# Finishing the all-node units of layers 2 and 3 earlier, and projecting front tiles first in layer 2

## The chip, the core and the metric

The kernel runs on one core of a Trainium2 chip. The core has a matrix engine (TensorE, PE in the profile; its weight loads are listed apart as PEld), a vector engine (VectorE, DVE), a scalar engine for functions such as exponentials (ScalarE, ACT), GpSimd (POOL), which here issues gathers, and SyncE (SP), whose queue issues the ordinary DMA transfers. The engines run side by side. Each takes its own instructions from its own list and they wait for one another on semaphores. The metric is the time of the whole kernel on the device in microseconds; the time before is 2346.93 us, the median of three runs (2338.59 to 2347.44).

## The reference

There are 4096 nodes with 256 features. The graph is a 4096 x 4096 adjacency matrix; an entry is set with a chance of 1 in 256, and the diagonal always. Four graph-attention layers follow one another, and each is wrapped in the same way:

```
x = layernorm(x + layer_n(x, adj))
```

Cut to its core, a layer does this for every node `i`:

```
h = x @ W
e[i, j] = leaky_relu(s[i] + d[j])          # s, d: h (or x) times short vectors
a[i, :] = softmax(where(adj[i, :], e[i, :], -inf))
out[i] = sum_j a[i, j] * h[j]
```

Layers 0 and 1 have four heads of 64 features and layer 2 has two heads of 128. Layer 3 has one head of 256 but two softmaxes, one of `e` and one of `-e`; both averages go through a matrix and `elu`. A node has some 16 neighbours, so the sum over `j` is sparse.

## The kernel before, in words

Nodes are handled in 32 row tiles of 128. For each row tile the kernel builds, during layer 0, a list of the nodes that are a neighbour of any of its 128 rows: 13 groups of 128 nodes. With the tile's own rows, which need no gather, that makes 14 positions. The six groups at the front hold only nodes of tiles 0 to 16 (`MIX = 17`), and these are called front nodes and front tiles here. The lists and masks are reused by all layers.

**A row tile** (`RowTile`) is worked in two halves of seven positions. `load` (lines 614 to 631) issues the DMA transfers of a half: for 13 positions of the 14 a gather on GpSimd (line 629) brings 128 rows of the projected values into a slot of the pool `g0` (16 slots; in layer 2 a slot holds two positions, so a tile takes 7; in layer 3 a slot holds one, and the second half's positions come from `g1`, 14 slots). The own rows come by SyncE's queue (line 626). `half` (lines 633 to 682) makes the weights: exponentials on ScalarE (line 670 in layer 2, lines 657 to 660 in layer 3), masks on VectorE (line 671, and 659 and 661), and then 14 matmuls on TensorE (line 682). After both halves, `finish` (lines 973 to 996) divides by the softmax sums on VectorE, adds the input and calls `norm` (lines 928 to 961), a chain of some twenty short VectorE instructions ending in line 956, which puts the tile into the list `ready`.

**All-node units** (`whole_rows`, lines 866 to 919) are a second way to compute the same thing. For the last `WHOLE[n]` blocks of four row tiles, the kernel doesn't gather: it runs over all 32 node tiles, with plain loads (line 888), exponentials over 512 columns (lines 900, and 903 to 907), one mask (lines 901 and 908), and matmuls (line 911). One node tile is a unit. Layer 2 has three such blocks, which makes 96 units of 8 matmuls, and layer 3 has one block, which makes 64 units of 4 matmuls (32 for each sign). So layer 2 has 20 row tiles with gathers and 12 without, layer 3 has 28 and 4. Gathers are GpSimd's work, and units need none.

**The order.** Layers 2 and 3 go through `half_with_whole` (lines 791 to 814) once for each half of a row tile: half step `2 m + part`. One half step makes at most one projection for the next layer (from `ready`, in the order of entry), one half of a row tile, the finish of the tile before, and as many units as `whole` (lines 736 to 742) allows: a share of all units that grows evenly and is complete 6 half steps before the layer's last one. After a block's last unit its four tiles are finished too and enter `ready`.

**A projection** (`Projection`, lines 520 to 591) takes a finished row tile to the values that the next layer gathers: transposes on TensorE (line 532), a copy on ScalarE (537), matmuls (546), an exponential (564), VectorE's part of the row (566 to 572) and the store of the row to HBM (574), and a small transposed store of its edge terms (578 to 585).

**The boundary.** `close` (lines 821 to 863) ends a layer: first the projections of front tiles that are left, then the first loads and gathers of the next layer, then the last tile's finish and the other projections. A gather of front groups needs the projected rows of tiles 0 to 16 only; any other gather needs those of all 32 tiles.

The Python loop isn't the last word: a scheduler places the instructions of each engine in an order of its own when the program is built, by readiness and its own estimates. On the chip each engine then keeps that order.

Of the kernel before, what the change touches and what calls it, by code (L numbers as in the profile page):

```python
# [76 lines left out]
MIX = 17  # L77
# [16 lines left out]


WHOLE = (0, 0, 3, 1)

LEAST = 2.0611536224385579e-09

# [35 lines left out]
def kernel(ctx: ExitStack, tc: tile.TileContext, ins: dict, out: bass.AP):  # L135
# [14 lines left out]
        "maskW": dram.tile([NB, P, NT, BT, MC], U8, name="maskW"),  # L150
        "d": [const.tile([P, NT, TERMS[n]], F32, name=f"d{n}") if WHOLE[n] else None for n in range(4)],
        "v": [dram.tile([N, ROW[n]], F32, name=f"vals{n}") for n in range(4)],
# [34 lines left out]
class Program:  # L187
# [97 lines left out]
    def lists(self, ctx):  # L285
# [71 lines left out]
        class Block:  # L357
# [24 lines left out]
            def places(self):  # L382
                blk = self.blk
                if blk >= NB - max(WHOLE):
                    nc.sync.dma_start(out=shared["maskW"][blk], in_=self.mk)
# [134 lines left out]
class Projection:  # L520
# [36 lines left out]
    def row(self):  # L557
# [8 lines left out]
        nc.vector.tensor_copy(self.terms[:, :, :A], st[:, :, :A])  # L566
        if WHOLE[n]:
            nc.vector.tensor_copy(sh["d"][n][:, m, :], st[:, 1, :])
# [136 lines left out]
class Layer:  # L705
# [3 lines left out]
    def __init__(self, prog, n):  # L709
        self.prog, self.n, self.nc, self.shared = prog, n, prog.nc, prog.shared  # L710
        self.count = NT - WHOLE[n] * BT
        self.tiles = {}
        self.loaded = set()
        self.units = self.whole_rows()
        self.total = WHOLE[n] * NT * (1 if n < 3 else 2)
        self.used = 0
# [18 lines left out]

    def whole(self, step):

        while self.used < self.total and self.used < self.total * (step + 1) / (2 * self.count - 6):
            next(self.units)
            self.used += 1  # L740
        if self.used == self.total:
            next(self.units, None)

    def part(self, m, part):


        if part == 0:
# [3 lines left out]
            for q in (m, m + 1):  # L751
                for half in range(2):
                    self.load(q, half)
        if WHOLE[self.n]:
            self.half_with_whole(m, part)
# [35 lines left out]
    def half_with_whole(self, m, part):  # L791

        proj = None
        self.step = 2 * m + part
        if self.ready and self.ready[0][0] < self.step:
            _, y, row = self.ready.pop(0)
            self.set_banks()
            proj = Projection(self.prog, self.n + 1, self.nxt, y, row)
            proj.transpose()
        if part == 1 or self.tile(m).accs is None:  # L800
            self.tile(m).half(part)
        if self.stored is not None:
            self.stored.store()
            self.stored = None
        if proj is not None:
            proj.copy()
            proj.multiply()
        if part == 1 and m >= 1:
            self.tile(m - 1).finish()
        self.whole(2 * m + part)  # L810
        if proj is not None:
            proj.row()
            proj.edge()
            self.stored = proj
# [643 lines left out]
```

## Time and profile before

| what | us |
|---|---|
| median of three runs | 2346.93 |
| span of the profiled run | 2346.8 |
| layer 2: first half's matmuls begin | 1364.7 |
| layer 2: last matmul of a unit ends | 1763.7 |
| layer 2: last gather ends | 1779.1 |
| layer 2: last matmul of a half ends | 1800.2 |
| layer 3: first gather (front groups) begins | 1811.6 |
| layer 3: gathers of the other groups begin | 1845.5 |
| layer 3: last matmul of a unit ends | 2287.0 |
| layer 3: last gather ends | 2311.0 |
| layer 3: last matmul ends | 2334.4 |

| engine | busy us | share of the span |
|---|---|---|
| TensorE, matmuls | 2052.4 | 87% |
| TensorE, weight loads | 1864.7 | 79% |
| VectorE | 1838.1 | 78% |
| ScalarE | 1747.3 | 74% |
| GpSimd | 1582.6 | 67% |

The shares are averages over layers that have different limits, so the table of times is the one to keep in mind: it cuts the last 1000 us at the places where something ends or begins. In a line of the timeline, the numbers are the start and the length in us; then follow the engine, the line of the kernel, the instruction with its output and inputs, how many were merged, and in brackets the idle time of the engine just before it with what ended it. An fp32 matmul of the code appears as two records.

### The profile page before, as it was taken

The numbers are of one execution on the slowest core, as the hardware profiler recorded it, in microseconds if no ns is written. First come the engines' busy times: TensorE is split into PE (matmuls) and PEld (weight loads), VectorE is DVE, ScalarE is ACT, GpSimd is POOL, SyncE is SP. The second block draws the span as 40 slices with busy tenths as digits, with TensorE's granted clock in tenths as the row PEclk, the third lists the DMA queues.
The fourth block names the chain that finished last, engine by engine and source line by source line (L and its number), as shares of the span: only waits on it lengthen the run. The fifth ranks groups of instructions, "written<-read, shape, count | busy, mean of one in ns | idle before, by whom it ended". The sixth has DMA issues, their size and how long they took to land.

```text
span 2346.8 us, 49828 instructions
## 1 busy us (share of the span) xinstructions
PE 2052.4 (87%) x15689; PEld 1864.7 (79%) x15689; DVE 1838.1 (78%) x6100; ACT 1747.3 (74%) x5137; POOL 1582.6 (67%) x1596
## 2 busy tenths in 40 slices
PE   4878898989988769999999889889898799979996
PEld 3668788888888759988888879888887688868885
DVE  3889999999987759989899859876866365656567
ACT  4779898897787749988888859877663666666663
POOL 2127887777788757777777767755553677777773
PEclk7999999999999979999999989999999899989998
DMA  8889687775555556666666657666665788888883
GB/s 278 267 269 322 220 284 255 245 268 155 157 140 159 148 168 182 190 176 170 174 175 183 167 147 202 200 187 188 187 179 150 248 250 276 268 245 267 272 251 119
DMA packets 250325, 492.01 MB, mean 210 GB/s; under 512 B 44385, under 2 KB 156610, under 8 KB 249666
## 3 DMA queue, kind: packets, MB, share of 16 engines
q0 software_dynamic: 81536, 245.30, 37.1%
q1 hardware_dynamic: 168514, 243.42, 32.5%
q8 instruction: 126, 2.06, 0.4%
q14 instruction: 149, 1.22, 0.2%
HBM read 436.24 MB, written 52.31 MB: 208 GB/s over the span
## 4 chain that ended last, share of the span: by engine, by line
PE 47%; DVE 20%; DMA 18%; ACT 8%; issue 4%; POOL 3%; SPq 0%; ACTq 0%; DVEq 0%; POOLq 0%
PE bank L679 17%; PE bank L682 12%; DMA G<-vals,idx 12%; PE bank L911 7%; PE bank L546 5%; DVE w L671 5%; PE bank L436 4%; DMA G<-vals 3%; POOL G L629 3%; DVE w L666 3%; DVE w L667 3%; ACT w L670 3%; DVE oh L430 2%; DMA raw<-in_adjB_dram 2%; ACT pw L900 1%
## 5 line engine op out<-in xcount | busy, mean ns | idle before, releaser
L629 POOL DMA_INDIRECT G<-vals,idx x1456 | 1569.6, 1078 | 718.5 <-issue 188.1
L670 ACT ACTIVATE w<-S,G 128x128 f32<-128x128 f32 x3248 | 1009.6, 391 | 204.7 <-DMA G<-vals,idx 194.6
L679 PE MATMUL bank<-w,G 128*65 128x128 f32 x7168 | 846.8, 279 | 94.9 <-DVE w L667 65.0
L679 PEld LDWEIGHTS bank<-w,G 128*65 128x65 f32 x7168 | 810.4, 142 | 109.8 <-DVE w L667 84.5
L682 PE MATMUL bank<-G,w 128*128 128x257 f32 (+1 forms) x2688 | 499.4, 344 | 34.8 <-ACT z L970 11.5
L682 PEld LDWEIGHTS bank<-G,w 128*128 128x128 f32 x2688 | 439.2, 196 | 84.7 <-ACT z L970 13.9
L671 DVE SCALAR_TENSOR_TENSOR w<-w,mk 128x896 f32<-128x896 f32 x272 | 292.6, 1082 | 42.8 <-ACT w L670 42.1
L911 PE MATMUL bank<-vw,pw 128*128 128x129 f32 (+1 forms) x2048 | 304.8, 306 | 14.3 <-ACT zw L970 13.0
L911 PEld LDWEIGHTS bank<-vw,pw 128*128 128x128 f32 x2048 | 279.4, 195 | 32.0 <-ACT zw L970 13.4
L666 DVE TENSOR_SCALAR w<-S,G 128x128 f32<-128x128 f32 x896 | 238.7, 298 | 80.0 <-DMA G<-vals,idx 78.9
L657 ACT ACTIVATE w<-S,G 128x128 f32<-128x128 f32 x392 | 137.9, 389 | 146.6 <-DMA G<-vals 96.6
L546 PE MATMUL bank<-wext,xT 128*128 128x268 f32 (+3 forms) x640 | 188.3, 427 | 49.7 <-ACT xT L537 45.9
L430 DVE TENSOR_SCALAR oh<-iota,place 128x256 bf16<-128x256 f16 (+2 forms) x992 | 223.7, 298 | 8.3 <-PE bank L436 7.9
L671 DVE SCALAR_TENSOR_TENSOR w<-w,bank 128x896 f32<-128x896 f32 x192 | 206.0, 1078 | 8.9 <-ACT w L670 8.8
L436 PE MATMUL bank<-mk,oh 128*128 128x132 fp8e4 x2336 | 188.7, 228 | 15.7 <-DVE oh L430 8.7
L436 PEld LDWEIGHTS <-oh 128*128 128x128 bf16 x2336 | 147.3, 100 | 51.3 <-DVE oh L430 23.5
L546 PEld LDWEIGHTS bank<-wext,xT 128*128 128x128 f32 x640 | 122.0, 208 | 72.8 <-ACT xT L537 50.8
L908 DVE TENSOR_TENSOR pw<-pw,mw 128x512 f32<-128x512 f32 x64 | 43.9, 690 | 137.8 <-ACT pw L907 71.2
L901 DVE SCALAR_TENSOR_TENSOR pw<-pw,mw 128x512 f32<-128x512 f32 x192 | 127.8, 687 | 21.2 <-ACT pw L900 19.8
L373 ACT ACTIVATE mk<-raw 128x1024 uint8<-128x1024 int32 x128 | 131.5, 1063 | 16.9 <-DMA raw<-in_adjB_dram 16.5
L900 ACT ACTIVATE pw<-Sw,d 128x512 f32<-128x512 f32 x192 | 132.9, 708 | 3.4 <-PE bank L911 3.2
L443 ACT ACTIVATE cm<-bank 128x384 uint8<-128x384 f32 (+1 forms) x160 | 70.1, 451 | 60.4 <-PE bank L436 58.4
(131 smaller groups left out, 1710.5 us busy)
## 6 DMA issues: line engine op xcount, KB each, us to landing
raw<-in_adjB_dram SPq DMA_DIRECT2D x128, 512.0 KB
mk<-maskC SPq DMA_DIRECT2D x112, 224.0 KB
G<-vals,idx POOLq DMA_INDIRECT x1456
S<-edge SPq DMA_DIRECT2D x64, 256.0 KB
vw<-vals SPq DMA_DIRECT2D x96, 129.0 KB
xp<-y SPq DMA_DIRECT2D x96, 128.0 KB
y<-xp SPq DMA_DIRECT2D x96, 128.0 KB
mw<-maskW SPq DMA_DIRECT2D x20, 528.0 KB
```

What stands on the lines that cost most here:

```text
L430: nc.vector.tensor_scalar(oh[:, :n * P], iota[:, :n * P], self.place[:, it, j:j + 1], None, op0=ALU.is_equal)
L436: nc.tensor.matmul(accs[b][:, s * MC:(s + 1) * MC], oh[:, (k - a) * P:(k - a + 1) * P], mk[:, j, it, :].bitcast(FP8), start=touches[b][0] ...
L546: nc.tensor.matmul(pp[:, :c1 - c0], self.xT[:, k, :], wext[:, k, c0:c1], start=(k == 0), stop=(k == KT - 1 and brow is None))
L629: nc.gpsimd.indirect_dma_start(out=self.place(pos), out_offset=None, in_=sh["v"][n][:NODES[t], :], in_offset=bass.IndirectOffsetOnAxis(ap= ...
L657: nc.scalar.activation(w[0][:, k, :], S[:, 0, :], AF.Relu, bias=d(k, 0))
L666: nc.vector.tensor_scalar(w[h][:, k, :], S[:, h, :], d(k, h), LEAST, op0=ALU.mult, op1=ALU.max)
L670: nc.scalar.activation(w[h][:, k, :], S[:, h, :], AF.Exp, bias=d(k, h))
L671: nc.vector.scalar_tensor_tensor(w[h], w[h], LEAST, mh, op0=ALU.max, op1=ALU.mult)
L679: nc.tensor.matmul(accs[0][:Wd, h * P:(h + 1) * P], v, w[h][:, k, :], **how)
L682: nc.tensor.matmul(a, w[h][:, k, :], v, **how)
L900: nc.scalar.activation(p, S[:, h], AF.Exp, bias=d)
L911: nc.tensor.matmul(accs[it][:, c:c + Wd], p[:, it, :], v[:, c:c + Wd], start=(j == 0 and h == heads[0]), stop=(j == NT - 1), skip_group_ch ...
```

## The change

The number of half steps that are left when the units are used up becomes one for each layer: 12 for layer 2 and 10 for layer 3, in place of 6 for both. The 96 units of layer 2 are then spread over 28 half steps (34 before) and the 64 of layer 3 over 46 (50 before). This is to have the blocks without gathers finished, and their tiles projected, before the layer's last tiles are. The second part concerns the choice of the next projection: among the tiles in `ready` that may go, front tiles are taken ahead of others (Python's sort keeps the order of entry among equals). It bears on layer 2 alone, since layer 3 projects nothing. It is to let the next layer's front gathers start without waiting for the rows of tiles 17 to 31. No instruction is added or removed; only their order differs.

```diff
 WHOLE = (0, 0, 3, 1)
+LAST = (0, 0, 12, 10)
...
     def whole(self, step):
 
-        while self.used < self.total and self.used < self.total * (step + 1) / (2 * self.count - 6):
+
+        while self.used < self.total and self.used < self.total * (step + 1) / (2 * self.count - LAST[self.n]):
             next(self.units)
             self.used += 1
...
         self.step = 2 * m + part
-        if self.ready and self.ready[0][0] < self.step:
-            _, y, row = self.ready.pop(0)
+
+        able = sorted((e for e in self.ready if e[0] < self.step), key=lambda e: e[2] >= MIX)
+        if able:
+            self.ready.remove(able[0])
             self.set_banks()
-            proj = Projection(self.prog, self.n + 1, self.nxt, y, row)
+            proj = Projection(self.prog, self.n + 1, self.nxt, *able[0][1:])
             proj.transpose()
```

## The prediction

> **What bounds the kernel now.** I read the chain of waits first: TensorE heads it (47%), by the matmuls of lines 679, 682 and 911, but gathers (line 629) stand in it too. A share over 2347 us says little about two stages, so I cut layers 2 and 3 into stretches.
>
> ```profile
> PE 47%; DVE 20%; DMA 18%; ACT 8%; issue 4%; POOL 3%; SPq 0%; ACTq 0%; DVEq 0%; POOLq 0%
> ...
> 1680.00:1750.00 70.00, 63.88 (x495) 60.73 (x494) 53.16 (x149) 50.55 (x135) 38.62 (x38) 0.95 0.63 179
> 1750.00:1790.00 40.00, 33.20 (x251) 31.36 (x251) 24.95 (x117) 18.82 (x60) 20.92 (x21) 0.96 0.57 163
> 1790.00:1820.00 30.00, 25.51 (x128) 19.92 (x127) 17.29 (x97) 9.53 (x24) 6.54 (x7) 0.89 0.53 158
> ...
> 2100.00:2200.00 100.00, 100.00 (x463) 87.67 (x462) 58.36 (x169) 63.81 (x136) 77.32 (x75) 1.00 0.88 270
> ```
>
> Columns: stretch, us, then busy time of PE, PEld, DVE, ACT, POOL, the granted clock, DMA share, GB/s. Layer 2 with units (to 1764) is TensorE's: 63.9 of 70 us, while GpSimd issued only 38 gathers. Layer 3 is another matter: 75 gathers in 100 us look like 77% busy, but GpSimd's own timeline shows 0.3 us between gathers and no longer rest; from 1845 to 2311 it starts 344 gathers in 466 us, 1.355 us each. The last gathers of layer 2 run at the same rate (11 in 14.6 us, 1.33 each):
>
> ```profile
> 1753.63 0.95 POOL L629 DMA_INDIRECT G<-vals,idx  x1 [0.30 <-issue]
> 1756.98 0.94 POOL L629 DMA_INDIRECT G<-vals,idx  x1 [2.41 <-issue]
> 1758.23 0.95 POOL L629 DMA_INDIRECT G<-vals,idx  x1 [0.31 <-issue]
> ...
> 1778.17 0.95 POOL L629 DMA_INDIRECT G<-vals,idx  x1 [0.30 <-issue]
> 1811.63 0.94 POOL L629 DMA_INDIRECT G<-vals,idx  x1 [32.51 <-ACT row L564]
> ```
>
> The last line is the boundary: GpSimd rests 32.5 us until tile 16, the last front tile, has its projected row in HBM. Eight projections follow one another there about 4.9 us apart (ScalarE's row exponentials, line 564, at 1786.25, 1791.56, 1796.50, 1801.97, 1806.31 and on), and the fifth of them is tile 16.
>
> The prices come from these rows, which count each fp32 matmul of the code twice:
>
> ```profile
> 1745.58 3.29 PE L682 MATMUL bank<-G,w 128*128 128x129 f32 x28
> 1748.71 5.53 PE L911 MATMUL bank<-vw,pw 128*128 128x129 f32 x48
> ```
>
> A half of layer 2 (14 matmuls) is 3.29 us, an all-node unit (8 matmuls) a third of 5.53, 1.84 us; a projection is 0.38 + 2.01 + 0.27 = 2.66 us (lines 532, 546, 578).
>
> **What the Trainium skill says.** "PSUM — Partial Sum Buffer", Engine vs sequencer instructions: the queues of ScalarE, VectorE and GpSimd are strict FIFO and matmuls complete in program order. The trace agrees: copies of line 537 stand behind exponentials that wait for gathers, and TensorE waits for them (6.05 us at 1491.6). So the order in which the built program puts instructions decides, not the order of the Python loop. "Perfetto Trace Analysis", What "DMA-bound" means: one of its kinds is an issuing engine whose track is solid with DMA slices, and those slices are descriptor generation. That is GpSimd in layer 3: 0.95 us and 0.3 us between. "DMA: Bandwidth & Descriptors", Anatomy of one DMA: some 2 us of a DMA are fixed, most of it the write's receipt, worst in HBM. Here the row of tile 16 is issued at 1807.46 and the first gather starts at 1811.63, 4.2 us later.
>
> **Part 1, the pace of layer 2.** Number half steps 0 to 39. Before, 96 units go over 34 of them, 80 in the first 28; after, all 96 are used in the first 28. Work is only moved, so while TensorE is the bound the moved work costs its own length. Half step 28 began at 1695.2 (first matmul of that half). Sixteen units more are 29.5 us, and 20 projections in place of 18 stand ahead of that point in the built order: 5.3 us. That gives 1730. TensorE was idle 40.6 us between 1375 and 1750, and denser units may fill a little: I take 1728 (1724 to 1732).
>
> Then twelve half steps run alone, where before six did. TensorE needs 12 x 3.29 + 3 projections = 47 us for them, ScalarE 12 x 4.2 (13 exponentials in 3.90). GpSimd: a tile takes 13 gathers, and the pool of 16 slots, 7 to a tile, lets it lead by a little over two tiles. At 1763.7, when the first of before's six lone halves started, 11 gathers were still to start, of tile 19. By the same lead, at half step 28 are left 11 of tile 16 and 3 x 13 of tiles 17 to 19: 50, at 1.35 us = 67 us. The last gather ends at 1795 in place of 1779.1. Bounds: 48 at 1.30 from 1724 is 1786 (+7); 51 at 1.39 from 1732 is 1803 (+24). So +16 us: six more halves lie where gathers set the pace and TensorE has nothing to put beside them.
>
> **Part 2, the boundary.** By the loop, after leaves two projections (18, 19) for the close where before leaves four (16 to 19): 9.8 us saved. The built order says otherwise. On VectorE the normalisation of the last block and of tiles 13 on stands among the weights (line 671) of later halves. After the last weight of layer 2 follow the rows of 29, 14, 30, 15, 31, 16, 17, 18, 19: nine, and before 28, 29, 30, 31, 16, 17, 18, 19: eight. The front sort even interleaves 14 and 15 with 30 and 31, so 16 is sixth, not fifth. One row more is 4.9 us; row 29 is further ready when the last exponential ends, where row 28 came 4 us after it. Net +2 us (0 to +5). Behind tile 16's row waits GpSimd's first front gather, behind tile 19's row every full gather; from there the order is as before. Layer 3 starts 18 us late (7 to 29).
>
> **Part 3, layer 3.** 64 units go over 46 half steps in place of 50. A half is 6.07 us, a unit 1.73, so a tile with units costs TensorE 12.14 + 2.78 x 1.73 = 16.95 us, before 16.57. GpSimd needs 13 x 1.355 = 17.6. The denser tiles are just hidden; I charge +2 us (0 to +5) for stalls that TensorE can no longer make up.
>
> The tail gains. Now the end of the last block falls among the last halves:
>
> ```profile
> 2286.87 12.30 PE L682 MATMUL bank<-G,w 128*128 128x257 f32 x56
> 2301.33 3.30 PE L682 MATMUL bank<-G,w 128*128 128x257 f32 x14 [2.17 <-ACT z L970]
> 2311.18 23.25 PE L682 MATMUL bank<-G,w 128*128 128x257 f32 x98 [6.54 <-DVE z L989]
> ```
>
> TensorE rests 8.7 us, because tile 24's finish (it frees the PSUM bank) is interleaved with the block's four on VectorE, then owes 98 records when the last gather ends at 2311. In the built order after, that block is finished four halves earlier. The last half then ends by its data: landing 3.7 us (the chain of waits), exponentials and masks 4.5 (0.4 + 0.85 + 0.94 + 2 x 1.09), matmuls 6: some 14 us after the last gather in place of 23.4. I take -10 us (-11 to -4). But there the stall falls while GpSimd still needs slots: the equal stall at 2076 to 2083 held it 5.8 us. I charge +3 (0 to +6). Layer 3 in sum: -5 us (-11 to +7).
>
> **Sum:** +16 + 2 + 2 - 10 + 3 = +13 us: 2360, 0.55% slower.
>
> **The rivals.** *The tail pays for the pace* (not slower): 48 gathers at 1.30 from 1724 (+7), +2, -10: 2346. For it: gathers back to back are 1.25 us, and layer 2's end carries less traffic. Against: every long stretch averages 1.33 or more. *The plan works as meant*: the boundary drops two projections (-9.8) and the tail -11: 2326. For it: projections do run in series there with TensorE half idle. Against: the built order has nine rows after the last weight, not two, and six more lone halves cost GpSimd something. *Both layers lose*: +18 and the tail's gain eaten by GpSimd's stall and by TensorE (+3): 2368. For it: layer 3 has two limits within 3% of each other.
>
> **How the numbers follow.** Forecast 2360: 0.40; both lose: 0.10; tail pays: 0.39; plan works: 0.11. Slower by over 0.5% means over 2358.7, the forecast and the last rival: 0.50. Faster means below 2335.2, the plan: 0.11. The rest is the same: 0.39. The range leaves out part of the plan and of the worst case: 2341 to 2372.
>
> **What would show it.** Right: the last unit of layer 2 on TensorE near 1728 (before 1763.7); GpSimd solid after it to about 1795; TensorE idle 15 us or more between; the first gather of layer 3 near 1830 and its full gathers near 1863 (before 1811.6 and 1845.5); 13 to 17 us from the end of layer 3's last gather to the end of its matmuls (before 23.4). Wrong, if the last gather of layer 2 still ends near 1780, if rows of tiles 14, 15 and 16 land while gathers still run, or if GpSimd pauses in layer 3 for over 10 us.

## The result, and the profile after

The changed kernel takes 2365.36 us (median of four runs, 2363.85 to 2372.15); the kernel before took 2342.76 us beside it (four runs, 2337.29 to 2347.44). The ratio of the runs is 1.0103, with a 95% interval from 1.0068 to 1.0137: 1% slower. The medians differ by 22.6 us. The profiled executions differ by 17.3 us (2364.1 and 2346.8), and the sums below are of those two.

Lines of `after` stand one further than before up to the unit quota, and four further in the half step: the gather is line 630, the half's matmul 683, the unit's 915, the row's store 575.

TensorE's timeline of the changed kernel where the units end (start, duration, then the instruction group; in brackets the idle time before it and what ended it):

```profile
1726.30 5.52 PE L915 MATMUL bank<-vw,pw 128*128 128x129 f32 x48
1731.65 0.27 PE L579 MATMUL bank<-ident,row 128*1 128x128 f32 x1
1731.76 3.29 PE L683 MATMUL bank<-G,w 128*128 128x129 f32 x28
...
1780.48 2.92 PE L683 MATMUL bank<-G,w 128*128 128x129 f32 x12 [5.25 <-ACT w L671]
1791.10 0.69 PE L533 MATMUL bank<-ident,y 128*128 128x128 f32 x2 [7.70 <-DVE u L957]
```

The last unit of layer 2 (line 915) ends at 1731.8; before it ended at 1763.7. The halves behind it (line 683) no longer follow one another: TensorE waits 5 us for a weight, and 8 us for a normalisation that stands on VectorE behind weights. The weights wait in turn. These are two lines of the waits of all engines between 1732 and 1803 us (who waited for what: us in total, times, the longest):

```profile
ACT w L671 <- DMA G<-vals,idx: 30.9, 26, 2.7
DVE w L672 <- ACT w L671: 29.7, 9, 5.4
```

ScalarE's exponentials wait 30.9 us for gathered rows, and VectorE's masks wait for those exponentials. GpSimd's timeline in the same stretch shows why the rows come late:

```profile
1755.15 0.95 POOL L630 DMA_INDIRECT G<-vals,idx  x1 [0.30 <-issue]
1756.40 0.95 POOL L630 DMA_INDIRECT G<-vals,idx  x1 [0.30 <-issue]
1762.02 0.94 POOL L630 DMA_INDIRECT G<-vals,idx  x1 [4.67 <-ACT w L671]
...
1801.68 0.95 POOL L630 DMA_INDIRECT G<-vals,idx  x1 [0.30 <-issue]
1836.05 1.11 POOL L630 DMA_INDIRECT G<-vals,idx  x1 [33.42 <-ACT pw L909]
...
1869.82 0.94 POOL L630 DMA_INDIRECT G<-vals,idx  x1 [7.41 <-issue]
```

Apart from one rest of 4.67 us it goes from one gather to the next with 0.3 us between, until 1802.6. 49 gathers start after the last unit. Then come the rest at the boundary, the first front gather at 1836.05, and the first gather that needs all tiles at 1869.82; before, these were at 1811.63 and 1845.48:

```profile
1845.48 0.94 POOL L629 DMA_INDIRECT G<-vals,idx  x1 [5.75 <-issue]
```

The stretches of the changed kernel (stretch, its length, then busy time of PE, PEld, DVE, ACT, POOL, the granted clock, DMA share, GB/s):

```profile
1728.00:1803.00 75.00, 48.34 (x327) 44.87 (x326) 39.56 (x178) 37.88 (x121) 54.38 (x53) 0.77 0.57 152
1803.00:1836.00 33.00, 26.74 (x159) 22.30 (x158) 20.73 (x116) 11.45 (x35) 0.00 (x0) 0.95 0.42 124
...
2100.00:2200.00 100.00, 100.00 (x463) 87.67 (x463) 56.10 (x163) 62.44 (x136) 76.89 (x76) 1.00 0.87 271
```

In the first, TensorE is busy for 48 of 75 us, VectorE for 40, ScalarE for 38, and GpSimd issues 53 gathers. So none of the other three is full. TensorE's 48 us are near the 47 that the prediction counted for its work there, and it is idle for 27, so the low granted clock of 0.77 is not what lengthens the stretch. In the middle of layer 3 nothing has changed: 463 matmul records and 76 gathers in 100 us (before 463 and 75).

Where the 17.3 us are, by differences of the two profiles:

| stretch | before | after | difference |
|---|---|---|---|
| start of the span to layer 2's first gather | 1350.6 | 1347.9 | -2.7 |
| from there to the end of its last gather | 428.5 | 454.7 | +26.2 |
| on to the first full gather of layer 3 | 66.4 | 67.2 | +0.8 |
| on to the end of layer 3's last gather | 465.5 | 468.9 | +3.4 |
| on to the end of layer 3's matmuls | 23.4 | 12.0 | -11.4 |
| on to the end | 12.4 | 13.4 | +1.0 |

The change does not touch the first stretch. In the profiles of all kernels on chips of this speed it lasts 1343.4 to 1355.3 us, so its -2.7 us are chance, and the change itself costs 20.0 us in this pair, nearer to the 22.6 of the medians.

### The profile page after: what moved, and what is told of

Read it like the earlier page. It is cut to its first block, busy times and chain, and to the rows that moved or that the text cites. A ratio compares the mean times of both kernels' runs of the same rounds, so it can differ in the third digit from the quotient of the medians.

```text
span 2364.1 us, 49868 instructions
## 1 busy us (share of the span) xinstructions
PE 2052.6 (87%) x15689; PEld 1863.9 (79%) x15689; DVE 1836.8 (78%) x6100; ACT 1754.3 (74%) x5137; POOL 1589.5 (67%) x1596
## 5 line engine op out<-in xcount | busy, mean ns | idle before, releaser
L915 PEld LDWEIGHTS bank<-vw,pw 128*128 128x128 f32 x2048 | 281.8, 196 | 30.7 <-ACT zw L974 12.4
L547 PE MATMUL bank<-wext,xT 128*128 128x268 f32 (+3 forms) x640 | 196.1, 441 | 59.4 <-ACT xT L538 56.0
```

The source lines that it names most:

```text
L547: nc.tensor.matmul(pp[:, :c1 - c0], self.xT[:, k, :], wext[:, k, c0:c1], start=(k == 0), stop=(k == KT - 1 and brow is None))
L915: nc.tensor.matmul(accs[it][:, c:c + Wd], p[:, it, :], v[:, c:c + Wd], start=(j == 0 and h == heads[0]), stop=(j == NT - 1), skip_group_ch ...
```

## The experiments

All kernels are edits of the kernel before; `LAST` is the number of half steps, by layer, that are left when the units are used up. Each was timed beside the kernel before. The theories were: the lone halves go at the pace of gathers (theory 1); the boundary's rows and their order cost the time (theory 2); layer 3's denser units cost it.

The first four ran on another chip than all others. The kernel before takes 2898.6 us there, so of these only ratios to before, and times within one profile, are used. The others ran on two chips of one speed.

### One part alone

```
# layer 2's units earlier and the front order, layer 3 as before
LAST = (0, 0, 12, 6)
```

> The change without its layer-3 part (12 for layer 2, 6 for layer 3, front tiles first). My theory: twelve lone halves of layer 2 run at the pace of the gathers, so the last gather of layer 2 ends 20 to 25 us later than before, the boundary keeps its length, and layer 3 keeps its old tail of 23 us after the last gather: 2343 + 24 = 2367, ratio 1.010. Rival: the loss comes from layer 3, whose denser tiles let GpSimd run out of slots: then this kernel is within 5 us of before.

Measured: 1.0055 (1.0036 to 1.0074). Layer 2's part costs time alone, though about half of what was expected.

```
# layer 3's units earlier, nothing else
LAST = (0, 0, 6, 10)
```

> Layer 3's part alone (6 for layer 2, 10 for layer 3, projections in the order of entry). My theory: the end of the last block leaves the last halves, the tail after the last gather shrinks from 23 to 12 us, and 3 us are given back in the denser part: 2343 - 8 = 2335, ratio 0.9965. Rival: the denser part costs as much as the tail gains, ratio 1.000, or the tail's gain seen in the changed kernel needs layer 2's part.

Measured: 0.998 (0.9958 to 1.0002). Layer 3's part is at best a small gain; 0.9965 was expected.

```
# the front order alone
LAST = (0, 0, 6, 6)
able = sorted((e for e in self.ready if e[0] < self.step), key=lambda e: e[2] >= MIX)
```

> Front tiles first, with 6 half steps left in both layers. In the built order tile 16's row is the second of eight after the last weight of layer 2 (before: the fifth), so the first front gather should start some 15 us after the last weight, 12 to 15 us earlier than before; the row of tile 19, which every other gather waits for, keeps its place. My theory: the gain is what the 21 front gathers (28 us) no longer lie behind: 0 to -8 us, ratio 0.9985. Rival: nothing is gained since tile 19's row sets the end of the boundary: ratio 1.000.

Measured: 0.9991 (0.9967 to 1.0014): no difference that can be measured. (The front gathers at a boundary are 20 in the traces, not 21.)

```
# both layers' units earlier, without the front order
LAST = (0, 0, 12, 10)
```

> The change without the sort (12 and 10, projections in the order of entry). In the built order five rows are left after the last weight of layer 2 (15 to 19), where the changed kernel has nine, and tile 16 is the second of them, not the sixth. Theory 1, gathers alone set the loss: the last gather of layer 2 stays at +23 us, the boundary shortens by 4 rows of 4.9 us at most, 2365 - 15 = 2350, ratio 1.003. Theory 2, the boundary's length is set by tile 19's row and by the front gathers, not by the rows ahead: 2362 or more, ratio 1.008.

Measured: 1.0002 (0.998 to 1.0023). This is below both theories' figures: here the whole change but the order costs nothing that can be measured, and this is where the other chip matters. Its page for the kernel with layer 3's part alone has, as the group of halves of layers 0 and 1:

```profile
PE 2304.1 (80%) x15689; PEld 2025.6 (70%) x15689; DVE 1852.7 (64%) x6100; ACT 1759.9 (61%) x5137; POOL 1544.2 (54%) x1596
...
L679 PE MATMUL bank<-w,G 128*65 128x128 f32 x7168 | 979.3, 297 | 206.0 <-issue 163.9
```

The same 7168 matmuls take 846.8 us in the profile of before, with 94.9 us of idle time ahead of them, most of it ended by VectorE; here 979.3 and 206.0, and most of the idle time is "issue", time for which the profile shows no wait. TensorE is slower there, and gathers are less of a limit: behind the last unit GpSimd rests five times for more than 1 us, 15.2 us in all, where the changed kernel on its chip rests once, 4.7 us. Counted from layer 2's first gather, the last one ends at 498.7 us, and at 485.7 in the kernel with layer 3's part alone, whose layer 2 is that of before: +13.0. From there to the first full gather, the first that needs all tiles, pass 54.5 us in place of 68.9: -14.4. The two cancel. The same kernel is run once more below, beside the others.

### Fewer gathers behind the units

```
# in place():
if n == 2 and self.m >= 14: pos -= pos % 2
# in load():
if n == 2 and m >= 14 and pos % 2: continue
```

This is added to the changed kernel. Tiles 14 to 19 of layer 2 then gather 6 of their 13 positions and read those rows twice, so 42 gathers are left out, with their transfers, and the engines other than GpSimd have the same work. Half of the rows it works with are then other nodes', so its output is not the layer's.

> The changed kernel, but in layer 2 the last six gathered tiles (14 to 19, the twelve lone half steps) gather only 6 of their 13 positions and read those rows twice; half of their gathered rows are therefore other nodes' rows. Theory 1, the lone halves run at the pace of the gathers: with 6 x 1.35 us a tile the gathers stop being the limit, ScalarE's 12 x 4.3 us remain, and the last weight of layer 2 comes 15 to 20 us earlier; the kernel is 12 to 20 us faster than the changed one. Theory 2, VectorE's order of projections sets the loss: less than 5 us come off.

Measured: 0.9947 (0.9929 to 0.9965), 2340.24 us, where the changed kernel took 2374.45 on the same chip (below): 34 us less. That is well over the 12 to 20 expected: counted from layer 2's first gather, the last weight is made 31.7 us sooner than there (429.6 and 461.3), not 15 to 20. The stretch from the last unit to the last gather, and to the first front gather:

```profile
1734.00:1775.00 41.00, 33.86 (x264) 32.42 (x263) 33.58 (x160) 29.61 (x101) 24.45 (x22) 0.93 0.60 159
1775.00:1813.00 38.00, 33.84 (x189) 28.42 (x188) 24.69 (x131) 14.98 (x47) 0.59 (x1) 0.90 0.41 122
```

TensorE is busy for 33.9 of 41 us in place of 48 of 75, at a granted clock of 0.93 in place of 0.77. The last unit ends at 1733.7, near the changed kernel's 1731.8, and the last gather at 1774.3.

The counterpart on the kernel before, for its six lone halves (tiles 17 to 19, `self.m >= 17` and `m >= 17`; 21 gathers left out):

> The control: the kernel before, with 6 of 13 gathers left in layer 2 for tiles 17 to 19, its six lone half steps. Theory 1: GpSimd leads by two tiles there and is hardly waited for, so 0 to 6 us come off, well under what the same edit takes off the changed kernel. Theory 2: as much as there, since the edit only takes GpSimd's and the DMA queues' work away.

Measured: 0.9986 (0.9969 to 1.0003), 2343.78 us, 5 us less than before, which is within the noise (7 us at the interval's end). A gather left out saves 34 / 42 = 0.8 us in the changed kernel and 5 / 21 = 0.24, at most 7 / 21 = 0.35, in the kernel before. Behind twelve lone halves gathers are the limit, behind six they nearly aren't. This supports theory 1 most directly. It does not part the issue of a gather on GpSimd from its transfer, since both were left out; for the issue speak GpSimd's timeline without rests and the DMA share of 0.57 in the changed kernel's stretch, where layer 3 has 0.87.

### The order with layer 2 as before

```
LAST = (0, 0, 6, 10)
able = sorted((e for e in self.ready if e[0] < self.step), key=lambda e: e[2] >= MIX)
```

> Front tiles first and 10 half steps for layer 3, with layer 2's 6 kept: the two parts that cost nothing by themselves. The tail after the last gather should be 12 us in place of 23, and the first front gather of layer 3 some 12 us earlier after the last gather of layer 2. If the two are independent: 6 to 10 us faster than before, ratio 0.9965. If the earlier front gathers only wait for tile 19's row: the tail's share alone, 0.998.

Measured: 0.9995 (0.9977 to 1.0013). GpSimd's timeline at the boundary:

```profile
1788.96 0.95 POOL L629 DMA_INDIRECT G<-vals,idx  x1 [0.30 <-issue]
1813.53 0.95 POOL L629 DMA_INDIRECT G<-vals,idx  x1 [23.62 <-DMA y<-xp]
...
1855.37 0.95 POOL L629 DMA_INDIRECT G<-vals,idx  x1 [16.20 <-DMA vals<-row]
```

The front gathers come 23.6 us after the last gather in place of 32.5, as the order means them to. But they are only 20, and the next gather then waits 16 us for the last row, which is stored 55.6 us after the last weight (before 53.7). What ends the boundary is the row of tile 19, and here this order did not make it earlier. In this profile the last gather itself also ends later, 435.3 us after layer 2's first in place of 428.5, so against the start of the layer the front gathers gain 2 us and the full ones lose 6; one profile of each does not say whether the order does that. Of the 6 to 10 us that the two parts were to save together, none was found.

### The changed kernel again

> The changed kernel again, on the chip of these runs, for comparison with them. Twelve lone halves at the pace of the gathers, one row more at the boundary, a shorter tail: ratio 1.005 to 1.010, and its last gather of layer 2 as late against the start of the layer as in the kernel with layer 2's part alone.

Measured: 1.0094 (1.0072 to 1.0115); the result repeats, and so does the last gather of layer 2, 454.9 us after its first (454.7).

### The number of lone halves

Four kernels without the front order, with layer 3's part, beside one another: `LAST = (0, 0, a, 10)` with a = 12, 9, 3 and 18.

> The change without the sort (12 and 10), beside other numbers for layer 2 on one chip. From the earlier runs: the last gather of layer 2 ends 26 us later against the layer's start than with 6, but only five projections are left after the last weight, so the last row comes 42 us after it in place of 54; layer 3 saves 3 us. Sum: +26 - 12 - 3 = +11 us, ratio 1.004 (changed kernel: 1.009). If the sort has no share: 1.009.

> 9 half steps for layer 2, 10 for layer 3, no sort. If each lone half beyond six costs what twelve cost, 26 / 6 = 4.3 us: +13; six rows after the last weight in place of eight: -8; layer 3 -3. Sum +2, ratio 1.001. If GpSimd's lead hides the first few lone halves more than the later: -2 to 0, ratio 0.9995.

> 3 half steps for layer 2, 10 for layer 3, no sort. Gathers: with 6 they were waited for over 5 us at the end (5 us came off when half of them were left out), so with 3 the last gather may end 5 to 10 us earlier; but the last block's end then falls into the close, with eight rows after the last weight as before: -5 to +5, and layer 3 -3. Ratio 0.997 to 1.001.

> 18 half steps for layer 2, 10 for layer 3, no sort: the suspected cost, doubled. Gathers set the pace of eighteen lone halves: six more than twelve, each 8.1 us by gathers against some 4 us by TensorE, so 26 us more: the last gather 52 us later than before. Four rows are left after the last weight (54 us less 4 x 4.2): -17. Layer 3 -3. Sum +32, ratio 1.0135. If the loss doesn't come from gathers but from the order of the projections, 18 is no worse than 12.

The second and third columns count from layer 2's first gather; "rows" is the number of projections behind the last weight of layer 2 in the built order:

| a | last gather ends | first full gather | rows | ratio (95%) |
|---|---|---|---|---|
| 3 | 424.3 | 493.7 | 8 | 1.0009 (0.9995 to 1.0022) |
| 6 (before) | 428.5 | 494.9 | 8 | 1 |
| 9 | 446.6 | 503.3 | 6 | 1.0034 (1.0013 to 1.0055) |
| 12 | 460.9 | 513.0 | 5 | 1.0051 (1.0033 to 1.0069) |
| 18 | 483.2 | 530.6 | 4 | 1.0139 (1.0111 to 1.0166) |
| 12 and the order (after) | 454.7 | 521.9 | 9 | 1.0103 (1.0068 to 1.0137) |

The cost grows with the number of lone halves, as theory 1 has it; between 3 and 6 it is nearly flat. The expectations for 3, 12 and 18 were met within the intervals. Nine cost more than either figure expected (1.001 and 0.9995): its last gather is 18 us later, not 13. With 18 the stretch after the last unit is long enough to be read alone:

```profile
1693.00:1829.00 136.00, 91.08 (x547) 83.17 (x545) 72.72 (x312) 73.31 (x232) 87.24 (x88) 0.85 0.57 164
```

GpSimd issues 88 gathers in 136 us, and TensorE is idle for 45 of the 136.

Theory 2 has its share as well, and the row with 12 and no order shows which. GpSimd's timeline of that kernel:

```profile
1809.67 1.18 POOL L629 DMA_INDIRECT G<-vals,idx  x1 [0.31 <-issue]
1830.26 0.95 POOL L629 DMA_INDIRECT G<-vals,idx  x1 [19.41 <-PE bank L682]
...
1862.93 0.94 POOL L629 DMA_INDIRECT G<-vals,idx  x1 [3.70 <-DMA vals<-row]
```

GpSimd rests 19.4 us, not 33.4, and the first full gather comes 52 us after the last gather of layer 2 in place of 67: five projections are left instead of nine, and the last row is stored 40.4 us after the last weight (54.3 in the changed kernel). The last gather ends 6 us later than in the changed kernel, so 521.9 - 513.0 = 9 us remain as the price of the order with twelve lone halves; the ratios, from three separate timings, say 1.0051 against 1.0094 and 1.0103, 10 to 12 us. On the slower chip the comparison can be made on one chip: with twelve lone halves the first full gather comes 564.6 us after layer 2's first with the order and 553.2 without, 11 us apart.

## Why the prediction was right, and where it was off

**The forecast** was 2360 us, slower, and measured were 2365.36. The direction, the stage and the limit were right. The size was not: +13 us were forecast, and measured were 20.0 in the profiles (17.3 with the chance of the first stretch) and 22.6 between the medians. That the time itself lies only 5 us off is partly luck: the forecast stood on 2346.93 for the kernel before, which took 4 us less beside the changed one. In the sum one term was too small by 10 us, and smaller ones gave some 3 of it back.

**The bound.** Layer 2 with units was read as TensorE's, its end as GpSimd's. The runs with fewer gathers show the second directly: 34 us for 42 gathers. It fits what the Trainium skill's "Perfetto Trace Analysis", What "DMA-bound" means, says of an issuing engine's solid track: POOL shows as 54.4 of 75 us busy, 73%, and still has one rest alone between gathers 0.3 us apart.

**Part 1, the pace, is the mis-sized term:** predicted +16 (7 to 24), measured +26.2 from layer 2's first gather, just outside the range, or +23.5 in absolute time. It has two halves:
- The last unit was to end at 1728, which is 377.4 us after the first gather in before's count; it ended at 1731.8, 383.9 after: +6.5. Two us had been deducted for idle time that denser units would fill, and they filled none: TensorE is idle for 40.8 us from the first gather to the last unit, and before it was for 38.1 up to half step 28. That is 4.7 us of the 6.5. The work moved ahead of this point took 36.7 us of TensorE where 34.8 were added, which is the rest. Copies of line 538 still hold TensorE up, as "PSUM — Partial Sum Buffer", Engine vs sequencer instructions, leads one to expect where a copy stands in ScalarE's strict order: 0.65 us and 1.90 us in the two projections at 1697.7 and 1712.2 alone.
- From there to the last gather 67 us were predicted (50 gathers of 1.35) and 70.8 measured. 49 gathers and 1.355 us are 66.4; the 4.4 us above that are the one rest of 4.67 us from 1757 to 1762, ended by an exponential (line 671). The count, one too many, and the price were right, and this rest was left out. That GpSimd waited for a slot there is the likely reading; the profile names only what ended it.

**Part 2, the boundary:** predicted +2 (0 to 5) for nine rows in place of eight, measured +0.8. SyncE's timeline of the stores shows why one row more cost so little:

```profile
1809.67 0.32 SPq L575 DMA_DIRECT2D vals<-row  x1
1813.86 0.32 SPq L575 DMA_DIRECT2D vals<-row  x1
1818.07 0.32 SPq L575 DMA_DIRECT2D vals<-row  x1
...
1830.72 0.32 SPq L575 DMA_DIRECT2D vals<-row  x1
...
1863.07 0.32 SPq L575 DMA_DIRECT2D vals<-row  x1
```

The first six come 4.2 us apart, where 4.9 was taken from before. The sixth (1830.72) is tile 16's by the built order, and the first front gather starts 5.3 us after it. The ninth (1863.07) is tile 19's, 6.8 us ahead of the first full gather. The claim that the built order, not the loop, decides held: nine rows, as counted there. What the prediction did not see is that the order itself was the cause of the nine. Without it five rows are left and the boundary takes 52 us. The +2 of this term are thus the difference of two larger effects: 14 us of saving by the earlier units, and what the order takes back, of which 9 are net, since without the order the last gather ends 6 us later.

**Part 3, layer 3:** predicted -5 (tail -10, denser tiles +2, a pause of GpSimd +3), measured -11.4 + 3.4 = -8.0. The tail is as worked out. TensorE's timeline of the changed kernel:

```profile
2275.54 12.30 PE L683 MATMUL bank<-G,w 128*128 128x257 f32 x56
2293.49 4.98 PE L683 MATMUL bank<-G,w 128*128 128x257 f32 x14 [5.65 <-ACT z L974]
2303.22 9.11 PE L683 MATMUL bank<-G,w 128*128 128x257 f32 x33 [4.76 <-DVE z L993]
...
2325.81 24.86 PE L683 MATMUL bank<-G,w 128*128 128x257 f32 x114
```

The rests at the block's finish (5.65 + 4.76 us) now end 35 us before the last gather's end (2338.7), and TensorE has caught up by then: its matmuls end 12.0 us after it, where 14 were predicted and 23.4 measured before. The pause of GpSimd that was charged for this place did not come in this profile, where it rests nowhere for more than 1.5 us from 2100 on; in four others with layer 3's part it rests once near the block's finish, for 3.3 to 4.8 us. (The charge was taken from a stall in mid-layer that was called equal; TensorE's rest there is 13.0 us, up to 2079.0, and not 8.7.) Instead the pause in mid-layer grew:

```profile
2094.45 1.20 POOL L630 DMA_INDIRECT G<-vals,idx  x1 [7.38 <-ACT e L997]
```

Before it was 5.81 us at 2088.72, and in the other kernels 5.6 to 10.7. So the +3.4 have 1.6 us of another place's pause in them, and the rest isn't resolved. Over all kernels with layer 3's part, those on the slower chip apart, layer 3 takes 468.9 to 474.2 us from full gathers to its last gather, with six left 464.8 and 465.5; so a third or more of the tail's gain is given back, and the part alone measures 0.998 and, with the order, 0.9995.

**The rivals.** "The tail pays for the pace" failed by the pace: +26, not +7. "The plan works as meant" has a true core, five projections instead of eight when the order is left out, but even then the ratio is 1.0051. "Both layers lose" gave 2368, closer to the time than the forecast, for a wrong reason in layer 3, whose gain was eaten only in part.

**The named signs.** Last unit near 1728: 1731.8. GpSimd solid to about 1795: to 1802.6, but for one rest. TensorE idle 15 us or more between: 75.0 - 48.3 = 26.7. First gathers near 1830 and 1863: 1836.0 and 1869.8. 13 to 17 us at the tail: 12.0. Of the signs of being wrong none came: the last gather of layer 2 ends 23.5 us later, the rows behind the last weight are all stored after the last gather, and no pause of GpSimd in layer 3 is over 7.4 us.

**What stays open.** Why single gathers in long stretches take up to 1.9 us where most take 0.95 wasn't found, and with it whether the pace of 1.355 us is GpSimd's alone. Why the scheduler puts the rows of tiles 14 to 16 and of the last block so late with the front order, and whether another order of the same work would keep five rows and early front gathers, was not tried. Of the kernels that compute the same as before none is clearly faster; the best ratio is 0.998, whose interval reaches 1.0002.

## What to carry to other kernels

Filler work that hides a slower side stream should last until the stream has little left: when it is used up early it is not saved but moved, and the halves left over go at the stream's pace (here 1.355 us a gather, so that the stream ended some 5 us later for each half step that was moved). Here six half steps without filler cost no more than three. Ask of every "sooner" at a boundary what ends it last; putting the front tiles first moved the front gathers 9 us nearer to the last gather of layer 2, and the full ones by 1 us. And count the built order, not the loop, for each part by itself and then for both together: the order cost nothing that could be measured with six lone halves and some 10 us with twelve.

## What the runs showed of the hardware

- One chip ran the kernel before in 2898.6 us, others in 2343 to 2349: 24% longer, with TensorE's waits put down to "issue" and a granted clock of 0.86 in place of 0.95. A change measured 1.0002 there and 1.0051 elsewhere, so a ratio from one chip need not hold on another.
- The granted clock was lowest in the stretches where TensorE had most gaps: 0.77 in the changed kernel's lone halves (busy 64%) and 0.85 in those of the kernel with eighteen (67%). In layer 3 (100%) it was 1.00. Between 81 and 91% busy the stretches shown have 0.89 to 0.96, in no order.
- From the issue of a row's store to the first gather that needs it passed 4.2 us before and 5.3 after for tile 16, and over all kernels 3.2 to 6.9 us for tile 19.
- GpSimd was the limit while its busy share read 73%: between two gathers, most of 0.95 us, lie 0.3 us even where it rests for nothing. In layer 3 it shows as 77% busy in that way.
